# Four conditioned transformer layers in one recorded schedule: values by twos, layer 3 rebuilt, minima, tables on GpSimd, and products of the identity in TensorE's waits

## The chip, the cores and the metric

The kernel runs on one core of one Trainium2 chip, in one launch. The metric is device time in microseconds (us), the median of the runs shown. The engines are TensorE (PE; its weight loads, PEld, are listed apart), VectorE (DVE), ScalarE (ACT), GpSimd (POOL), and SyncE (SP), whose queue issues most DMAs.

## The reference, cut to what matters

Four layers follow each other on x of shape (4, 512, 512), all in float32; a conditioning vector of 512 numbers per batch element scales and shifts inside them.

```
# layer 0: attention, 16 query heads of 32, 4 key heads; keys and values through a latent of 128
h = layernorm(x) * (1 + scale) + shift           # scale, shift from the conditioning
q, k = rope(h @ Wq.T), rope((h @ Wkd.T) @ Wku.T); v = (h @ Wkd.T) @ Wvu.T
x = x + softmax(masked(q k^T / sqrt(32))) v @ Wo.T      # a window of +-64 and every 64th key
# layer 1: attention, 8 query heads of 64, one key head; then a gated MLP of 2048
h = rms(x) * w * (1 + scale);   x = x + softmax(rope(q) rope(k)^T / 8) v @ Wo.T
h = rms(x) * w2 * (1 + scale2); x = x + (silu(h @ Wg.T) * (h @ Wu.T)) @ Wd.T
# layer 2: attention with normalized q and k, 16 heads of 32, an additive bias; then an MLP of 2048
q, k = q / |q| * sm, k / |k|;   x = x + (softmax(q k^T + bias) v @ Wproj.T + bproj) * gamma1
x = x + (gelu_tanh(h @ Wfc1.T + bfc1) @ Wfc2.T + bfc2) * gamma2
# layer 3: 8 experts on slices of 64 features, then a projection
y = gelu(x_e @ W1[e] + b1[e]) @ W2[e] + b2[e]            # e = 0..7, hidden 256
hn = (layernorm(y) * g + b) * (1 + scale) + shift
x = x + silu(hn) @ out_W + out_b
```

## The kernel before, in words

**Two streams, one recorded order.** Each of the four batch elements passes the stages `a01` (attention of layers 0 and 1), `m1` (MLP of layer 1), `a2` (attention of layer 2) and `m2` (MLP of layer 2 and the experts of layer 3). Two streams run side by side: `STREAM_A` holds mostly attentions, `STREAM_M` mostly MLPs. At the start both are in `a01`, of elements 1 and 0; at the end element 3's experts are done in two halves, one per stream. The stages are Python generators. They yield a cost, or an `Until`, which says when a buffer is written or free. `interleave` picks the next step of a stream, and the class `Clocks` keeps a plan: it knows about when each engine will be done with each tile. Every instruction is recorded with its planned start and emitted sorted by it, so that the order on each engine is written out before the kernel runs and nothing reorders it on the chip. Where no step is ready, `interleave` moves the planned time of TensorE (`clocks.now`) forward to the earliest `Until`.

**Lines of the profile.** All work goes through four helpers, so line numbers tell the helper and the tile names tell the step: L301 is every operation of VectorE, ScalarE and GpSimd, L354 every matrix product (`mm`), L360 every transpose by TensorE (`tr`, a product with the identity `ident`), L367 the loads on SP's queue (`load`).

**Tiles.** 512 tokens are 4 tiles of 128 rows. Stream A's names are `nq` (normalized input, then transposed queries), `h`, `probs`, `pT`, `kT`, `v`, `wa_*` (weights); stream M uses `mn`, `mT`, `wm`, `hid`, `x` and `wm_*` for the same things. A side has two PSUM banks of its own, `bank`; scores go to `two`, two pairs of banks that both sides share. `late` is a scratch of VectorE, then a ring of conditioning weights, then the additive bias of layer 2.

**Attention.** A unit is one block of heads (`c`) and one tile of queries (`qt`). `attention` goes through the units: it issues the scores of the next unit, then `back` transposes the probabilities of this one (TensorE into a bank, copied to `pT` by `evict`, which takes ScalarE or VectorE, whichever the plan has free first), and `values` multiplies `pT` by `v` into a bank, evicted to `ctxT`. The list `late` holds units whose values are outstanding; with two in it the older is done:

```
            if len(late) == 2:
                yield Until(*when, side.at, of=late[0][1])
                values(*late.pop(0))
```

Scores use a quarter (32 rows) or a half (64) of the array, four or two at a time; values a quarter or half of the columns.

**Softmax.** `maxima` adds the bias and takes the row maximum on VectorE, negates it in a second operation, and `soften` lets ScalarE exponentiate with it and sum, VectorE invert the sums and GpSimd multiply.

**Tables.** `tables` and `trig` make sines and cosines for rope with some 20 operations; table "0" (128x64) and table "1" (128x512) both on VectorE, at the start. The conditioning weights are loaded into `late` after table "1".

**Layer 2's q, k, v** are made in that order, four token tiles each; q and k are squared on ScalarE, summed on VectorE, and scaled on GpSimd. **Layer 3** (`experts`) adds the first bias in `first` on VectorE and ScalarE, applies Gelu in place over all of `hid`, transposes back in `third`, normalizes, turns with `turned`, applies Silu in place, and projects.

Of the kernel before, what the change touches and what calls it, by code (L numbers as in the profile page):

```python
# [12 lines left out]
F32 = mybir.dt.float32  # L13
# [11 lines left out]
LOWEST = -3.0e38  # L25
# [283 lines left out]
def cond_seq_kernel(ctx: ExitStack, tc: tile.TileContext, a: dict, out: bass.AP):  # L309
# [89 lines left out]

    class Side:  # L400
# [8 lines left out]
        def bank(self):  # L409
            return clocks.tile(self.row_tag + "bank", 2, self.pools[0], (P, 512), "bank", name("bank"))  # L410

        def at(self, k=1):

            return clocks.free(self.row_tag + "bank", 2, k)
# [12 lines left out]
    class AttentionSide(Side):  # L427
# [28 lines left out]
        def pair(self):  # L456
            t = two_banks()
            return [t[:, 0, :], t[:, 1, :]]

        def pair_at(self):  # L460
            return clocks.free("two", 2)

    class OtherSide(Side):
# [25 lines left out]

        def pair(self):  # L490
            return [self.bank(), self.bank()]

        def pair_at(self):
            return self.at(2)
# [72 lines left out]
    def trig(ang, k, e, sin, nsin, cos):  # L567


        r = ang  # L570

        def nearest(period):
            vector.tensor_scalar(k, r, 1.0 / period, MAGIC, ALU.mult, ALU.add)
            vector.tensor_scalar(k, k, -MAGIC, None, ALU.add)

        def less(part):
            vector.scalar_tensor_tensor(r, k, -part, r, ALU.mult, ALU.add)

        far = TWO_PI * 2.0**17
        big = split(far, 2.0**8, 12, 2)  # L580
        nearest(far)
        less(big[0])
        less(big[1])
        vector.tensor_scalar(e, k, big[2], None, ALU.mult)
        nearest(TWO_PI)
        for part in split(TWO_PI, 2.0**-4, 7, 4):
            less(part)
        vector.tensor_tensor(r, r, e, ALU.subtract)
        nearest(TWO_PI)
        for part in split(TWO_PI, 2.0**-9, 12, 2):  # L590
            less(part)
        vector.tensor_scalar(r, r, PI_F32, -PI_F32, ALU.min, ALU.max)
        scalar.activation(e, r, AF.Abs)
        scalar.activation(sin, r, AF.Sin)
        scalar.activation(cos, e, AF.Sin, bias=half_pi, scale=-1.0)
        vector.tensor_scalar(nsin, sin, -1.0, None, ALU.mult)

    def tables(label, n, half, tokens, freqs):
# [3 lines left out]
        vector.tensor_tensor(  # L602
# [5 lines left out]
        parts = [const.tile([P, n * half], F32, name=f"{label}_{i}") for i in range(3)]  # L608
        trig(ang, k, e, *parts)
        return [t.rearrange("p (t i) -> p t i", i=half) for t in parts]  # L610
# [31 lines left out]
    def norm_steps(n, src, eps, rms=False, tiles=range(NT)):  # L642

        mv, own = tiny([P, NT, 2], "mv"), slice(tiles[0], tiles[-1] + 1)
        for t in tiles:
            st = tiny([P, 6], "st")
            vector.bn_stats(st, src[:, t, :])
# [83 lines left out]
    def maxima(p, s, bias, width, scale):  # L731

        mx = tiny([P, 2], "mx")
        for j in range(2):
            vector.tensor_tensor_reduce(
                out=p[:, j, 0:width], in0=s[:, j, 0:width], in1=bias, scale=scale, scalar=LOWEST,
                op0=ALU.add, op1=ALU.max, accum_out=mx[:, j : j + 1],
            )
        neg = tiny([P, 2], "neg")
        vector.tensor_scalar(neg, mx, -1.0, None, ALU.mult)  # L740
# [4 lines left out]
    def attention(side, units, scores, back, values, work, first, final=True):  # L745
# [15 lines left out]

        yield Until(scorable, of=first)
# [3 lines left out]
        for i, u in enumerate(units):  # L766
            cost, more = 0.0, i + 1 < len(units)
            when = [scorable] if more else []
            if len(late) == 2:
                yield Until(*when, side.at, of=late[0][1])  # L770
                values(*late.pop(0))
                cost += work[1]
            else:
                yield Until(*when)
# [9 lines left out]
        for u, pT in late:  # L784
            yield Until(side.at, of=pT)
            values(u, pT)
            yield work[1]
# [81 lines left out]
    coefs, tabs, ended = {}, {}, set()  # L869
# [16 lines left out]
    def attention0(b, side):  # L886
# [4 lines left out]
        if "0" not in tabs:  # L891
            tabs["0"] = tables("tab0", NT, 16, tok, freq[:, 32:48])
# [61 lines left out]
        def scores(u):  # L954
# [11 lines left out]
            for q, sc in zip(p, s):  # L966
                neg = maxima(q, sc, bias, n, 1.0 / math.sqrt(32.0))
                soften(q, q, neg, n, 1.0)
# [19 lines left out]
        def values(u, pT):  # L988
            c, qt = u
            (pT,), o, bl = pT, side.bank(), blocks(qt)  # L990
            for i, (at, n) in enumerate(bl):
                for g in range(4):
                    mm(
                        o[quarter(g), 0:P], lhsT=v[0:n, qt, i, quarter(g)],
                        rhs=pT[0:n, i, g * P : (g + 1) * P], start=i == 0, stop=i == len(bl) - 1,
                    )
            evict(ctxT[:, c, qt * P : (qt + 1) * P], o[:, 0:P])

        if "1" not in tabs:

            posf = const.tile([P, B * NT], F32, name="posf")
            vector.tensor_copy(posf, pos_i)
            tabs["1"] = tables("tab1", B * NT, 32, posf, freq[:, 0:32])
            ringC.load(1)
# [6 lines left out]
    def attention1(b, side):  # L1011
        n, wkv1 = side.n(), (yield from unit_for(b, "wkv1"))
        norm(n, xs[b], 1e-6, rms=True)
        yield from known("n1")
        hT = side.h()
# [66 lines left out]
        def values(u, pT):  # L1082
            c2, qt = u
            o = side.bank().rearrange("p (i q) -> p i q", q=P)
            for i in range(2):
                for at in range(NT):
                    for j in range(2):
                        mm(
                            o[half(j), i, :], lhsT=v[:, at, :], rhs=pT[i][:, j, at, :],
# [599 lines left out]
```

## Time and profile before

| | |
|---|---|
| median of 3 runs | 2498.31 us (2492.44 to 2498.45) |
| the profiled execution | 2497.25 us |
| its span, first to last instruction | 2495.5 us |
| TensorE | 2432.5 us busy (97%), 12564 instructions |
| VectorE, ScalarE, GpSimd | 1190.5, 877.6, 733.5 us busy |
| mean granted clock of TensorE | 0.992 |
| moved by DMA | 154.18 MB, 62 GB/s on average |

A product in float32 is two records in the profile, a transpose is one. Busy times count a record from its start to its modelled end, so two records that overlap count once. An idle time is put down to the instruction whose semaphore ended it. A time before or after the span (1.75 us here) belongs to the execution as well.

### The profile page before, as it was taken

The page shows a single profiled execution, that of the slowest core. Times are in us where ns is not written, and L with a number is a line of the kernel's source. Part 1 is how long each engine was busy: PE and PEld are TensorE (multiplying, and loading weights), DVE is VectorE, ACT ScalarE, POOL GpSimd, SP SyncE. Part 2 cuts the span into 40 slices and gives each one's busy share as a digit, 9 for nine tenths or more (in the row PEclk, how much of TensorE's full clock was granted, in tenths as well). Part 3 has the DMA queues.
Part 4 walks back from the last instruction along what each step waited for, and adds up shares of the span by engine and source line. Part 5 has one row for each costly group of instructions (what it writes and reads, how often), then busy time and mean ns, then how long its engine had stood idle before and what let it go on. Part 6 is the DMA issues. An engine that isn't in the chain of part 4 may idle for free.

```text
span 2495.5 us, 33420 instructions
## 1 busy us (share of the span) xinstructions
PE 2432.5 (97%) x12564; PEld 1242.0 (50%) x12564; DVE 1190.5 (48%) x3180; ACT 877.6 (35%) x2071; POOL 733.5 (29%) x921
## 2 busy tenths in 40 slices
PE   7989999999999999999999999999999999999997
PEld 4555655444554555554455455554455444554443
DVE  6766552133654454625554455443465333763233
ACT  2645441002551351414353043333255202651233
POOL 2433320005332223324222232424332205533221
PEclk9999999999999999999999999999999999999998
DMA  3220122220113111111211111112111221102210
GB/s 112 100 74 18 52 68 68 86 87 34 35 52 106 51 52 55 39 68 55 89 48 61 63 69 65 42 56 72 68 35 52 83 89 53 44 32 95 72 55 21
DMA packets 83312, 154.18 MB, mean 62 GB/s; under 512 B 3584, under 2 KB 10784, under 8 KB 83152
## 3 DMA queue, kind: packets, MB, share of 16 engines
q1 hardware_dynamic: 82544, 151.83, 17.9%
q8 instruction: 100, 1.64, 0.3%
q14 instruction: 60, 0.49, 0.1%
q0 software_dynamic: 176, 0.15, 0.1%
q10 hardware_dynamic: 432, 0.07, 0.0%
HBM read 147.83 MB, written 4.21 MB: 61 GB/s over the span
## 4 chain that ended last, share of the span: by engine, by line
PE 88%; DVE 3%; issue 3%; ACT 2%; POOL 2%; DMA 1%; ACTq 0%; POOLq 0%; DVEq 0%
PE bank L354 71%; PE bank L360 11%; PE two L354 6%; POOL inv L301 1%; ACT probs L301 1%; DVE probs L301 1%; ACT wm L301 0%; DVE neg L301 0%; POOL t L301 0%; DVE pT L301 0%; DMA late_ada_g<-in_units 0%; DMA wm<-in_units 0%; DVE t L301 0%; DMA late_ada_t<-in_units 0%; POOL probs L301 0%
## 5 line engine op out<-in xcount | busy, mean ns | idle before, releaser
L301 POOL TENSOR_SCALAR probs<-probs,inv 128x512 f32<-128x512 f32 (+4 forms) x544 | 316.4, 596 | 688.4 <-DVE inv L301 579.4
L301 ACT ACTIVATE probs<-probs,neg 128x512 f32<-128x512 f32 (+2 forms) x448 | 265.4, 594 | 254.8 <-DVE neg L301 254.3
L360 PEld LDWEIGHTS bank<-ident,probs 128*128 128x128 f32 (+2 forms) x1744 | 201.9, 141 | 161.9 <-issue 128.6
L360 PE MATMUL bank<-ident,probs 128*128 128x128 f32 (+2 forms) x1744 | 245.4, 276 | 4.1 <-ACT arow L301 1.2
L354 PE MATMUL bank<-mT,wm_gate 128*128 128x512 f32 x512 | 248.9, 597 | 0.0
L354 PE MATMUL bank<-mT,wm_up 128*128 128x512 f32 x512 | 245.7, 597 | 0.0
L354 PE MATMUL bank<-wm_down,hid 128*128 128x512 f32 x512 | 239.6, 596 | 0.7 <-DVE hid L301 0.7
L301 DVE CUSTOM_DVE_ANT_0 probs<-two,late 128x512 f32<-128x512 f32 x256 | 166.2, 686 | 74.3 <-PE two L354 56.4
L354 PE MATMUL bank<-wm_fc,hid 128*128 128x512 f32 x384 | 187.6, 594 | 0.0
L354 PE MATMUL bank<-mT,wm_fc 128*128 128x512 f32 x384 | 182.6, 597 | 0.0
L301 ACT COPY pT<-bank 128x512 f32<-128x512 f32 (+2 forms) x240 | 133.8, 580 | 83.8 <-PE bank L360 75.8
L354 PEld LDWEIGHTS bank<-pT,v 128*32 128x32 f32 (+2 forms) x3488 | 110.7, 116 | 95.9 <-issue 33.3
L354 PE MATMUL bank<-pT,v 128*32 128x128 f32 (+2 forms) x3488 | 146.0, 278 | 8.3 <-DVE pT L301 5.8
L301 ACT ACTIVATE mt<-bank 128x512 f32<-128x512 f32 x64 | 37.8, 591 | 327.6 <-PE bank L354 327.6
L354 PE MATMUL bank<-wa_q,h 128*128 128x512 f32 x320 | 152.4, 599 | 0.2 <-DVE t L301 0.2
L301 DVE TENSOR_TENSOR x<-x,bank 128x512 f32<-128x512 f32 x100 | 68.4, 684 | 176.1 <-PE bank L354 176.0
L354 PE MATMUL two<-kT,nq 32*128 32x512 f32 (+5 forms) x1088 | 150.0, 539 | 1.1 <-DVE mx L301 1.1
L354 PEld LDWEIGHTS bank<-wm_down,hid 128*128 128x128 f32 x512 | 91.7, 190 | 98.1 <-issue 96.2
L354 PEld LDWEIGHTS bank<-mT,wm_up 128*128 128x128 f32 x512 | 91.0, 190 | 98.2 <-issue 97.7
L301 DVE RECIPROCAL inv<-total 128x2 f32<-128x2 f32 x320 | 53.0, 166 | 172.9 <-ACT probs L301 155.7
L354 PEld LDWEIGHTS bank<-mT,wm_gate 128*128 128x128 f32 x512 | 90.0, 190 | 90.8 <-issue 90.3
L301 DVE COPY pT<-bank 128x512 f32<-128x512 f32 (+2 forms) x199 | 131.1, 680 | 5.9 <-PE bank L360 5.0
(221 smaller groups left out, 3396.3 us busy)
## 6 DMA issues: line engine op xcount, KB each, us to landing
wm_fc<-in_units SPq DMA_DIRECT2D x24, 1024.0 KB, 5.6
wm_gate<-in_units SPq DMA_DIRECT2D x16, 1024.0 KB, 5.7
wm_up<-in_units SPq DMA_DIRECT2D x16, 1024.0 KB, 5.7
wm_down<-in_units SPq DMA_DIRECT2D x16, 1024.0 KB, 5.4
wa_q<-in_units SPq DMA_DIRECT2D x10, 1024.0 KB, 5.5
wa_fc<-in_units SPq DMA_DIRECT2D x8, 1024.0 KB, 5.5
wa_o<-in_units SPq DMA_DIRECT2D x6, 1024.0 KB, 5.7
wa_k<-in_units SPq DMA_DIRECT2D x4, 1024.0 KB, 5.6
```

What stands on the lines that cost most here:

```text
L301: return call(*map(real, args), **{k: real(x) for k, x in kw.items()})
L354: latest[0] = nc.tensor.matmul(real(out), lhsT=real(lhsT), rhs=real(rhs), **kw)
L360: latest[0] = nc.tensor.transpose(real(out), real(src), unit)
```

## The change

The new parts, each with what it does:

- `attention` does the values of two units together, when both have their `pT`; each `values` writes both into one bank (256 columns) and evicts once.
- `maxima` becomes `lowest`: scores times minus the scale, the row minimum; it goes to the exponential as it is (`scale=-1.0`), and the negation is gone.
- `trig` and `tables` take an engine and yield between operations. Table "0" stays on VectorE; table "1" goes to GpSimd as a list of `chores`, one operation at a time, whenever its input is ready in the plan. [...] Layer 1 of element 0 and the loads of the conditioning weights wait for that table.
- Layer 2's products come as q0 to q3, k0, k1, v0, k2, v1, k3, v2, v3; k is evicted by the freer engine, and VectorE does the scaling.
- Layer 3: `first` takes pairs of `two` on both sides and lets Gelu read PSUM with its bias; statistics are taken per block of 128 columns as they come; Silu becomes z(1 + tanh z) with z half of the input (the coefficients are halved once), per block.
- A side may take a bank of `two` for its own work when no attention is in its scores and its own banks are free later.
- `keep_up`: before `interleave` moves the planned time forward by a wait, it issues products of the identity with itself into a free bank, as many as fit the wait less 0.4 us at 0.215 us each, when that is at least two. Nothing reads them. The changed program has 117, in 21 places.

```diff
 class Side:
         def bank(self):
+            if not scoring and clocks.now < self.own() > clocks.free("two", 2):
+                return two_banks()[:, 0, :]
+            return self.own_bank()
...
+    def trig(ang, k, e, sin, nsin, cos, engine):
...
         def less(part):
-            vector.scalar_tensor_tensor(r, k, -part, r, ALU.mult, ALU.add)
+            if engine is vector:
+                vector.scalar_tensor_tensor(r, k, -part, r, ALU.mult, ALU.add)
+            else:
+                engine.tensor_scalar(sin, k, -part, 1.0, ALU.mult, ALU.mult)
+                yield Until(of=[sin])
+                engine.tensor_tensor(r, r, sin, ALU.add)
+            yield Until(of=[r])
...
-    def maxima(p, s, bias, width, scale):
-        mx = tiny([P, 2], "mx")
+    def lowest(p, s, bias, width, scale):
+        neg = tiny([P, 2], "neg")
         for j in range(2):
             vector.tensor_tensor_reduce(
-                out=p[:, j, 0:width], in0=s[:, j, 0:width], in1=bias, scale=scale, scalar=LOWEST,
-                op0=ALU.add, op1=ALU.max, accum_out=mx[:, j : j + 1],
+                out=p[:, j, 0:width], in0=s[:, j, 0:width], in1=bias, scale=-scale, scalar=HIGHEST,
+                op0=ALU.add, op1=ALU.min, accum_out=neg[:, j : j + 1],
             )
-        neg = tiny([P, 2], "neg")
-        vector.tensor_scalar(neg, mx, -1.0, None, ALU.mult)
         return neg
...
     def attention(side, units, scores, back, values, work, first, final=True):
...
             if len(late) == 2:
-                yield Until(*when, side.at, of=late[0][1])
-                values(*late.pop(0))
-                cost += work[1]
+                yield Until(*when, side.at, of=late[0][1] + late[1][1])
+                values(late)
+                late = []
+                cost += 2 * work[1]
...
     def attention0(b, side):
         if "0" not in tabs:
-            tabs["0"] = tables("tab0", NT, 16, tok, freq[:, 32:48])
+            for _ in tables("0", NT, 16, tok, freq[:, 32:48], vector):
+                pass
+            posf = const.tile([P, B * NT], F32, name="posf")
+            vector.tensor_copy(posf, pos_i)
+            chores.append(tables("1", B * NT, 32, posf, freq[:, 0:32], gpsimd))
...
     def attention2(b, side):
-        for which, dst in (("q2", qT), ("k2", kT)):
+        for which, t in [("q2", 0), ("q2", 1), ("q2", 2), ("q2", 3), ("k2", 0), ("k2", 1)] + [
+            x for i in range(2) for x in (("v2", i), ("k2", i + 2))
+        ] + [("v2", 2), ("v2", 3)]:
...
-                gpsimd.tensor_tensor(qv, qv, inv.unsqueeze(2).to_broadcast([P, 16, 32]), ALU.mult)
+                vector.tensor_tensor(qv, qv, inv.unsqueeze(2).to_broadcast([P, 16, 32]), ALU.mult)
...
-        def values(u, pT):
-            c, qt = u
-            o = side.bank()
-            for at in range(NT):
-                for g in range(4):
-                    mm(
-                        o[quarter(g), 0:P], lhsT=v[:, at, c * P + 32 * g : c * P + 32 * g + 32],
-                        rhs=pT[g // 2][:, g % 2, at, :], start=at == 0, stop=at == NT - 1,
-                    )
+        def values(two):
+            o, (c, first) = side.bank(), two[0][0]
+            for k, (_, pT) in enumerate(two):
+                for at in range(NT):
+                    for g in range(4):
+                        mm(
+                            o[quarter(g), k * P : (k + 1) * P],
+                            lhsT=v[:, at, c * P + 32 * g : c * P + 32 * g + 32],
+                            rhs=pT[g // 2][:, g % 2, at, :], start=at == 0, stop=at == NT - 1,
+                        )
...
     def experts(b, side, tiles=range(NT)):
-                for j in range(2):
-                    bias = V_B1 + 4 * p + 2 * j + f
-                    if j == 0:
-                        vector.tensor_scalar(at(j, f), s[j][:, 0:n], vec[:, bias : bias + 1], None, ALU.add)
-                    else:
-                        scalar.activation(at(j, f), s[j][:, 0:n], AF.Identity, bias=vec[:, bias : bias + 1])
-            for h in hid:
-                scalar.activation(h[:, :, 0:n], h[:, :, 0:n], AF.Gelu)
+            for f in range(2):
+                for j in range(2):
+                    bias = V_B1 + 4 * p + 2 * j + f
+                    scalar.activation(at(j, f), bank(j, f), AF.Gelu, bias=vec[:, bias : bias + 1])
...
+            for t in tiles:
+                vector.bn_stats(stats[:, t, p, :], y[:, t, p * P : (p + 1) * P])
...
-        yield from turned(side, y, hT, b, coefs["gain"], coefs["lift"], tiles)
-        scalar.activation(hT[:, :, lo : lo + n], hT[:, :, lo : lo + n], AF.Silu)
+        for c in range(NC):
...
+            scalar.activation(h, ps, AF.Tanh, bias=lift, scale=gain)
+            vector.tensor_scalar(z, ps, gain, lift, ALU.mult, ALU.add)
+            vector.scalar_tensor_tensor(h, h, 1.0, z, ALU.add, ALU.mult)
...
+    def keep_up(until):
+        start = max(clocks.now, clocks.written(ident))
+        count = int((until - start - 0.4) / 0.215)
+        if count > 1:
+            rings = [] if scoring else [("two", two_banks)]
+            rings += [(side.row_tag + "bank", side.own_bank) for side in (sideA, sideM)]
+            for ring, make in rings:
+                if clocks.free(ring, 2) <= start:
+                    p = make()
+                    p = p[:, 0, 0:P] if ring == "two" else p[:, 0:P]
+                    for _ in range(count):
+                        mm(p, lhsT=ident, rhs=ident, start=True, stop=True)
+                    break
...
             elif cond and cond_until.time < min(s.until for s in live):
+                keep_up(cond_until.time)
                 clocks.now = cond_until.time
             else:
                 s = min(live, key=lambda s: s.until)
+                keep_up(s.until)
                 clocks.now = max(clocks.now, s.until)
                 s.step()
```

## The prediction

> **What bounds the kernel now.** I read the page first, then busy time by stretches, then TensorE's timeline in the middle, then the clock around the slow stretches, then the tail. The page gives the bound:
>
> ```profile
> PE 2432.5 (97%) x12564; PEld 1242.0 (50%) x12564; DVE 1190.5 (48%) x3180; ACT 877.6 (35%) x2071; POOL 733.5 (29%) x921
> PEclk9999999999999999999999999999999999999998
> ```
>
> TensorE (PE) is busy 97% of 2495.5 us, no other engine half of it: PE is idle for 63.0 us. The stretches tell where (columns: stretch and its length, then busy us and count of PE, weight loads, VectorE, ScalarE, GpSimd; the granted clock; DMA share; GB/s):
>
> ```profile
> 0.00:100.00 100.00, 83.06 (x518) 48.19 (x522) 69.61 (x237) 41.53 (x125) 34.84 (x68) 0.98 0.33 100
> 100.00:200.00 100.00, 89.94 (x825) 54.11 (x816) 66.25 (x321) 55.80 (x208) 38.48 (x87) 0.97 0.23 78
> 200.00:300.00 100.00, 94.59 (x679) 58.35 (x679) 57.92 (x136) 47.52 (x128) 35.54 (x52) 0.98 0.13 43
> 300.00:400.00 100.00, 94.35 (x628) 57.00 (x625) 48.75 (x92) 39.07 (x97) 22.68 (x33) 0.98 0.13 43
> 400.00:1100.00 700.00, 698.21 (x3254) 349.92 (x3253) 304.50 (x797) 198.59 (x492) 171.82 (x217) 1.00 0.19 64
> ...
> 2400.00:2496.00 96.00, 81.50 (x289) 36.01 (x287) 31.60 (x61) 29.16 (x47) 21.56 (x18) 0.90 0.08 28
> ```
>
> Idle are 38.1 us in the first 400 (two attentions side by side, VectorE 49 to 70% busy), 14.0 in the tail, and only 10.9 in the 2000 us between. There the end moves by what PE's own work costs. The timeline shows that this is more than products (start, length, group; the next start matters, since lengths hold a tail of 0.17):
>
> ```profile
> 611.02 10.47 PE L354 MATMUL bank<-wa_v,h 128*128 128x512 f32 x24
> 621.33 0.60 PE L360 MATMUL bank<-ident,t 128*128 128x128 f32 x4
> ...
> 640.28 2.74 PE L354 MATMUL bank<-mT,wm_up 128*128 128x512 f32 x6
> 642.95 1.08 PE L354 MATMUL bank<-pT,v 128*32 128x128 f32 x32
> 643.96 1.14 PE L354 MATMUL two<-kT,nq 32*128 32x512 f32 x8
> 645.03 1.09 PE L360 MATMUL bank<-ident,probs 128*128 128x128 f32 x8
> ```
>
> 24 records from 611.02 to 621.33 are 0.429 us each, two to a product of 512 columns: 0.86. Values (pT,v) and scores (kT,nq) fill the array four at a time, so each of these two groups is worth 0.86 too; but from start to next start they take 1.01 and 1.07. The excess, 0.15 and 0.21, is paid where products of one tile size (128*128, 128*32, 128*64, 32*128, 64*128) follow another. I call it a switch. By kind its median in the trace is 0.15 to 0.22; before has 663, worth 127 us. Products at steady rates are 2260 us; the rest of the busy time is slow clock and tails.
>
> **Switches: the main term.** Values by twos halve the groups of values: 160 before, 80 after, each with the same products. A scores-then-values round had three switches; every other round now has two. In the order of the changed program PE has the same 7674 products and transposes plus 117 fillers, and 522 switches. Each kind's count times its median gives 127.2 before, 101.8 after: **-25.4**. Nearly all of it lies where PE does not wait, so it is on the path. Ends: 141 fewer at 0.15 or at 0.21, -21 to -30.
>
> What it adds is a wait: both units' pT, the second transposed just before. The copy to pT takes 0.59 on ScalarE or 0.68 on VectorE, with 0.17 of PE's tail and hops about 0.95. Queued behind on PE is everything, as its order is fixed. But in that order at least 1.05 us of PE's work stands between the pair's last transposes and its first value product for 79 of the 80 pairs, mostly two products of the other stream (1.72); the 80th has 0.46. I take 0; without that cover it costs 80 x 0.95 = 76. Halved copies of values leave VectorE and ScalarE, beside PE.
>
> **Fillers and the clock.** 117 products of the identity, in 21 places: 23 before the first product, 3 before the first product of q0, 37 in 8 places of the two-attention phase, 18 in 4 places of the middle, 36 in 4 places at the end. Each is two records of 128 columns, so 0.215 at full clock, 0.43 at half. The clock in stretches of one window, same columns, each pair before and in a slow one:
>
> ```profile
> 60.60:64.00 3.40, 1.92 (x10) 0.63 (x8) 3.33 (x14) 2.19 (x6) 1.26 (x1) 1.00 0.66 216
> ...
> 347.30:350.70 3.40, 0.77 (x8) 0.53 (x5) 3.09 (x8) 2.90 (x9) 1.08 (x2) 1.00 0.00 0
> ```
>
> ```profile
> 64.00:67.40 3.40, 3.15 (x9) 1.73 (x8) 3.05 (x17) 2.31 (x11) 2.38 (x5) 0.50 0.27 98
> ...
> 350.70:354.10 3.40, 3.35 (x32) 3.28 (x32) 0.68 (x2) 0.47 (x1) 1.61 (x3) 0.50 0.02 5
> ...
> 2473.80:2487.50 13.70, 8.37 (x15) 3.80 (x16) 2.55 (x7) 3.47 (x4) 0.71 (x1) 0.50 0.00 0
> ```
>
> A stretch with PE 0.77 to 1.92 of 3.4 us busy is followed by 3.4 us at 0.50. There are six such stretches before the tail (23.9 us, PE busy 23.6 of it) and 13.7 in the tail (busy 8.4). Half of the busy time is lost: 11.8 + 4.2. The first weight products, 16 records in 8.70 us at 22.76, lose 8.70 - 6.87 = 1.8. In all 17.8. The fillers stand in just such waits, but shorter waits have none: I take **-12**, ends 0 and -18.
>
> [...] The trace shows 0.50 after single waits of at most 2.7 us. [...]
>
> A filler that starts while the next operand is already there delays everything by itself. The identity is ready at 1.4 us and the first product starts at 9.27; 23 fillers between them take 4.9 at full clock, 9.9 at half, so at half they end 2.0 late: I take 1. The 91 after these 26 cost 19.6 at full clock; their cover is the waits of PE, and I take a tenth, 2. Together **+3**, ends 0 and +22.
>
> **Tables on GpSimd.** For layer 1 VectorE drops 10 operations at 0.69, 8 at 0.42, 2 at 0.69 and one at 0.43: 12.1 us between 24 and 60. GpSimd gains 10 at 1.27 and 17 at 0.60: 22.9 in the same phase, where it is busy 35 to 38%; its rope sums (1.27) and softmax products queue behind one such step at a time, up to 1.3 each. Conditioning's loads now wait for the tables, and SP's queue has them later; what needs all coefficients, layer 2, comes after 600 us.
>
> **Minima, and the start's waits.** The minimum in place of the maximum drops 256 negations at 0.17 and puts the result straight before ScalarE's exponential. No row shows the min form; its nearest, the max form, is 0.69 at 512 columns, and I take the same. In the middle it is beside PE. In the first 400 us, 64 of them (11 us) and the tables' 12 leave VectorE, 23 of its 242 busy us, a tenth. Waits there, 38.1 idle less 9.3 before the first product, are 28.8; a tenth of these is 3, and free "two" banks that a side may now use when nobody scores remove some more: **-8**, ends +10 (GpSimd's queue) and -20.
>
> **Layer 2's order, layer 3.** PE waits 2.0 us near 1165 and 1763 for GpSimd's scaling of k (1.05 on GpSimd, 0.69 on VectorE after). Values products between the k tiles cover a part, but fillers still stand there: 0. Layer 3 drops VectorE's additions and ScalarE's in-place pass; Gelu reads PSUM, four at about 0.59 (nearest row, Tanh from PSUM), 2.4, in place of an addition of 0.6 and one Gelu of 1.91: the consumer gets it as late as now, and PE has the other stream. Its "two" pairs are shared with scores; ends -3 and +8, taken 0. Only the tail is bare:
>
> ```profile
> 2471.53 0.44 PE L360 MATMUL bank<-ident,t 128*128 128x128 f32 x2 [0.22 <-DVE t L301]
> ...
> 2472.41 0.69 DVE L301 BATCH_NORM_STATS2 st<-nq 128x6 f32<-128x512 f32 x1 [0.94 <-ACT nq L301]
> ...
> 2479.11 1.28 ACT L301 ACT_TABLE_LOAD   x1 [0.49 <-DVE h L301]
> 2480.40 1.06 ACT L301 ACTIVATE h<-h 128x1024 f32<-128x1024 f32 x1
> 2481.51 10.07 PE L354 MATMUL bank<-wm_out,h 128*128 128x512 f32 x16 [3.06 <-ACT h L301]
> ```
>
> Two statistics of 0.69 shrink to two of 128 columns (between 0.17 and 0.69). From the first transposes to the last products 4.8 pass now; after: load 1.28, four Tanh at 0.56, one step of 0.5, 4.0. Together **-1**, ends -2 and +1.
>
> **Sum.** -25.4 - 12 + 3 - 8 - 1 = -43.4 against the profiled execution of 2497.25 (span 2495.5): 2453.9. It is 1.1 under the median of 2498.31, so about **2455**.
>
> **Rivals.**
> 1. *Values wait for the newest pT* (slower). At 0.95 for a bare pair, 80 bare cost 76: 2455 + 76 = 2531. It decides from 43.4 / 0.95 = 46 bare pairs of 80. For it: the wait is real. Against: 1.05 or more at 79 pairs. 0.06.
> 2. *Fillers are bare.* 91 x 0.215 = 20 instead of 3, and the clock gains little: -25 - 6 + 20 - 1 = -12, with the start unchanged: 2486. For it: nothing on PE can pass them. Against: in before, waits of 1 to 4 us stand at the same steps. 0.12.
> 3. *The clock is not theirs to raise*: the stretches at 0.50 follow waits too short for a filler, and 0 to 4 of the 12 come: 2463 to 2467. For it: a wait under about 0.8 gets none. Against: most slow stretches follow a longer one. 0.15.
> 4. *The start opens up*: waits there fall by 20 rather than 8, all slow stretches go: 2455 - 12 - 6 = 2437. For it: VectorE is busiest there. 0.17.
> 5. The change not doing what it says is left out by the order: 80 groups, 522 switches, 117 fillers are in it.
>
> **Numbers.** My case, 2446 to 2463, has 0.50. A range from 2434 to 2481 leaves out the slower rival, half of rival 2 and the far end of 4, under 0.2. The measurement of this kernel tells about 0.3%, 7.5 us, from no change. Faster by more: 0.50 + 0.17 + 0.15 + 0.09 = 0.91; within: 0.04 (rivals 1 and 2 in part); slower: 0.05.
>
> **What would show it.** Right: a pT,v group of 64 records taking about 1.87 to the next start, idle PE unchanged in the middle, the clock at 1.00 through 64, 350 and 1767 and in the tail, PE's busy sum lower by some 20 although 25 of fillers are in it. Wrong: waits of bank<-pT,v for ScalarE or VectorE copies above 10 us in all; fillers directly followed by products that waited for nothing; slow stretches that remain; GpSimd's queue ending waits of the softmax in the first 100 us.

## The result, and the profile after

| | before | after |
|---|---|---|
| median of 6 runs (lowest to highest) | 2494.90 us (2491.28 to 2498.45) | 2477.23 us (2475.66 to 2481.23) |
| ratio, 95% interval | | 0.9932 (0.9917 to 0.9946) |
| profiled execution, its span | 2497.25, 2495.5 | 2475.82, 2474.0 |

The change gains 17.7 us where 43 were forecast: right in its sign, 22 us from the number, and outside 2446 to 2463, which had half the chance. The first section of the page gives busy time and instructions by engine, the line below it the granted clock in 40 slices:

```profile
PE 2427.1 (98%) x12798; PEld 1278.0 (52%) x12798; DVE 1124.0 (45%) x2903; ACT 864.5 (35%) x2075; POOL 726.6 (29%) x920
PEclk9999999999999999999899999999999999999999
```

TensorE's sum fell by 5.4, not by some 20, and there is a new slow slice, the twentieth. The stretches (length, then busy us and count of PE, weight loads, VectorE, ScalarE, GpSimd; granted clock; DMA share; GB/s) show where:

```profile
0.00:100.00 100.00, 91.23 (x664) 56.88 (x664) 62.08 (x238) 48.55 (x151) 65.34 (x109) 0.97 0.30 90
...
400.00:1100.00 700.00, 696.99 (x3271) 352.77 (x3270) 297.11 (x733) 200.36 (x490) 169.54 (x214) 1.00 0.18 62
1100.00:1200.00 100.00, 87.95 (x312) 42.80 (x311) 40.48 (x85) 30.73 (x50) 29.10 (x14) 0.93 0.23 77
1200.00:2400.00 1200.00, 1194.55 (x6108) 606.10 (x6107) 542.07 (x1326) 424.16 (x937) 356.58 (x412) 1.00 0.18 61
2400.00:2474.00 74.00, 64.30 (x316) 36.58 (x314) 24.19 (x59) 23.64 (x53) 13.04 (x12) 1.00 0.06 22
```

Between 1100 and 1200 TensorE is idle for 12 us at a mean clock of 0.93. The same stretch of before:

```profile
1100.00:1200.00 100.00, 96.87 (x330) 43.95 (x329) 44.80 (x85) 35.12 (x45) 43.70 (x26) 1.00 0.15 53
```

TensorE's waits of after (tile, releaser: us in total, times, longest) say that it is one wait:

```profile
PE bank L360 <- DVE t L301: 12.7, 4, 11.6
PE bank L360 <- DVE pT L301: 6.0, 20, 0.3
PE two L354 <- ACT hid L301: 3.1, 3, 1.9
```

Its cause is three queues away. TensorE's timeline of after has the last products of the keys (`wa_k`), ended at about 1171.6, and the wait for `t`, the scaled keys:

```profile
1168.01 3.60 PE L354 MATMUL bank<-wa_k,h 128*128 128x512 f32 x8
1178.75 1.88 PE L354 MATMUL bank<-mT,wm_up 128*128 128x512 f32 x4
1192.26 1.09 PE L360 MATMUL bank<-ident,t 128*128 128x128 f32 x4 [11.63 <-DVE t L301]
```

VectorE, which makes `t`, stood for 15.89 at the statistics of `x`, the next element's input, which are ahead of it in VectorE's order:

```profile
1169.54 0.69 DVE L301 TENSOR_TENSOR t<-t,inv 128x512 f32<-128x512 f32 x1 [3.02 <-POOL inv L301]
1186.12 0.69 DVE L301 BATCH_NORM_STATS2 st<-x 128x6 f32<-128x512 f32 x1 [15.89 <-DMA x<-in_x]
```

And `x` was late because of SP's queue, where it stood behind a load that waited:

```profile
1129.94 0.37 SPq L367 DMA_DIRECT2D wa_v<-in_units  x1
1171.64 0.37 SPq L367 DMA_DIRECT2D wa_proj<-in_units  x1
1172.10 2.73 SPq L301 DMA_DIRECT2D out<-x  x4
1180.68 0.39 SPq L367 DMA_DIRECT2D x<-in_x  x1
```

Nothing was issued between 1130 and 1171: `wa_proj` overwrites the keys' weights, and with keys and values interleaved the last key product ends only then (1168.01 and 3.60 above). Behind it stood the four stores of element 0, and behind these the load of element 3's `x`, which takes element 0's place and so waits until the stores have landed. The load had been recorded when the values' weights are taken, before the last two key products were planned, so the plan held the buffer for free and put the load ahead of the stores.

### The profile page after: what moved, and what is told of

The parts are those of the page before. It is cut to its first block, busy times and chain, and to the rows that moved or that the text cites. A ratio compares the mean times of both kernels' runs of the same rounds, so it can differ in the third digit from the quotient of the medians.

```text
span 2474.0 us, 33722 instructions
## 1 busy us (share of the span) xinstructions
PE 2427.1 (98%) x12798; PEld 1278.0 (52%) x12798; DVE 1124.0 (45%) x2903; ACT 864.5 (35%) x2075; POOL 726.6 (29%) x920
## 4 chain that ended last, share of the span: by engine, by line
PE 93%; DVE 3%; ACT 2%; issue 1%; DMA 1%; POOL 0%; SPq 0%; DVEq 0%; ACTq 0%; POOLq 0%
PE bank L354 70%; PE two L354 11%; PE bank L360 11%; DVE probs L301 1%; DVE pT L301 1%; PE two L360 0%; ACT probs L301 0%; ACT wm L301 0%; DVE nq L301 0%; DMA out<-x 0%; DMA x<-in_x 0%; DMA wm<-in_units 0%; DVE mt L301 0%; ACT pT L301 0%; ACT L301 0%
## 5 line engine op out<-in xcount | busy, mean ns | idle before, releaser
L354 PE MATMUL bank<-mT,wm_gate 128*128 128x512 f32 x512 | 247.8, 595 | 0.0
L354 PE MATMUL bank<-mT,wm_up 128*128 128x512 f32 x512 | 246.9, 599 | 0.0
L354 PE MATMUL bank<-wm_down,hid 128*128 128x512 f32 x496 | 232.5, 597 | 0.0
L354 PE MATMUL bank<-wm_fc,hid 128*128 128x512 f32 x384 | 189.5, 593 | 0.0
L354 PE MATMUL bank<-mT,wm_fc 128*128 128x512 f32 x384 | 183.0, 595 | 0.0
L301 ACT COPY pT<-bank 128x512 f32<-128x512 f32 (+3 forms) x258 | 145.2, 577 | 81.1 <-PE bank L360 72.3
L354 PE MATMUL two<-kT,nq 32*128 32x512 f32 (+5 forms) x1088 | 149.7, 537 | 0.4 <-DVE neg L301 0.4
L354 PEld LDWEIGHTS bank<-mT,wm_up 128*128 128x128 f32 x512 | 91.3, 191 | 100.1 <-issue 99.6
L354 PEld LDWEIGHTS bank<-pT,v 128*32 128x32 f32 (+2 forms) x3488 | 113.0, 116 | 49.0 <-issue 20.9
L354 PEld LDWEIGHTS bank<-mT,wm_gate 128*128 128x128 f32 x512 | 90.5, 190 | 91.3 <-issue 91.3
L354 PEld LDWEIGHTS bank<-wm_down,hid 128*128 128x128 f32 x496 | 89.0, 190 | 94.2 <-issue 92.9
L301 POOL TENSOR_TENSOR inv<-ss,neg_half 128x16 f32<-128x16 f32 x32 | 92.8, 2901 | 131.1 <-DVE ss L301 131.1
L354 PE MATMUL bank<-pT,v 128*32 128x128 f32 (+2 forms) x3488 | 130.4, 274 | 0.0
L301 POOL TENSOR_TENSOR rstd<-var,neg_half 128x4 f32<-128x4 f32 (+1 forms) x25 | 24.7, 992 | 359.3 <-DVE var L301 359.1
L354 PE MATMUL bank<-wa_q,h 128*128 128x512 f32 x272 | 129.9, 596 | 0.0
```

Of the source, the lines that this page charges most:

```text
L301: return call(*map(real, args), **{k: real(x) for k, x in kw.items()})
L354: latest[0] = nc.tensor.matmul(real(out), lhsT=real(lhsT), rhs=real(rhs), **kw)
```

## Experiments

In the tables a difference is between two medians, each of 4 to 11 runs whose spread is 2 to 8 us; below 2 us it tells nothing. The runs were made in several rounds, in which before itself had medians of 2493.4 to 2495.8; differences of the ratios to before are within 1.4 us of those in the tables. "Useful work" is the sum of TensorE's steady durations without fillers (0.429 us per record of 512 columns, times the share of the array that its tile fills), 2256 us in every version. Compared at equal useful work, a profile tells in which stage a difference arose.

**First four: the wait, and two parts alone.**

`a_hold_k`, in the ring's bookkeeping:

```diff
 weights[which] = side.ring.take(which)
+if which == "k2":
+    side.ring.held[side.ring.taken - 1] = which
...
+if which == "k2" and t == NT - 1:      # after the last key product
+    side.ring.held = {at: x for at, x in side.ring.held.items() if x != "k2"}
+    side.ring.load(side.ring.taken + 1)
```

> The changed kernel, where the buffer of the key weights of layer 2 counts as held until the last key product is recorded; so the load of the projection weights (wa_proj) into it stands behind the four stores of element 0 and the load of x for element 3 in SP's queue, not ahead of them. Theory A (SP's queue: a load that waits 41 us for TensorE stood at its head, x of element 3 came late and VectorE's statistics with it): the wait of 11.6 us of bank<-ident,t at 1180 goes, with it the slow clock of 1183 to 1197 (about 2): about 2463 us, 12 to 14 below the changed kernel; the load of x lands before 1170. Rival B (VectorE's order itself, the statistics standing ahead of layer 2's keys, is what costs): x lands earlier, yet the wait stays above 8 us and the time within 4 of the changed kernel, 2474 or more.

`a_qkv_order`:

```diff
-for which, t in [("q2", 0), ... ("k2", 1)] + [x for i in range(2) for x in (("v2", i), ("k2", i + 2))] + ...
+for which, t in [(w, i) for w in ("q2", "k2", "v2") for i in range(NT)]:
```

> The changed kernel, where layer 2's products come in the old order again (q0 to q3, k0 to k3, v0 to v3); scaling on VectorE and all else stay. Theory A (the new order of q, k, v is what put the load of the projection weights in front of SP's queue): the wait of 11.6 us near 1180 goes, but the waits of TensorE for the scaled k (about 2 us in each of three middle elements, partly taken by fillers) come back: 2466 to 2470. Rival B (the order is not the cause): the long wait stays, 2477 or more.

`b_twos`: the kernel before with the new `values` and `yield Until(..., of=late[0][1] + late[1][1])`.

> The kernel before, with values by twos alone; 568 switches of tile size instead of 663 by its order. Theory A (a switch costs TensorE 0.15 to 0.21 us wherever TensorE does not wait): 95 x 0.17 = 16 less, about 2479. Rival B (the pairs wait for the newer pT and give it back): 2486 to 2495, with waits of bank<-pT,v for ScalarE or VectorE of 8 us or more in all. Rival C (a switch costs nothing of its own, the longer group is only a tail in the records): 2492 to 2495, with no such waits.

`b_fill`: the kernel before with `keep_up` and its two calls.

> The kernel before, with the products of the identity alone (150 in 29 places, into a side's own banks only). Theory A (they keep the granted clock up in the middle and in the tail, and some delay the next product): stretches at 0.50 near 350, 1767 and 2453 to 2487 gone, about 9 us, less 2 to 4 where they are bare: 2486 to 2489. Rival B (bare): no gain or slower, 2494 to 2505, with fillers followed at once by products that waited for nothing. Rival C (the clock follows something else): the stretches at 0.50 stay, 2492 to 2500.

| | median | ratio to before |
|---|---|---|
| after | 2477.23 | 0.9932 (0.9917 to 0.9946) |
| a_hold_k | 2464.92 | 0.9877 (0.9863 to 0.9891) |
| a_qkv_order | 2464.22 | 0.9881 (0.9865 to 0.9897) |
| b_twos | 2487.46 | 0.9972 (0.9961 to 0.9983) |
| b_fill | 2490.02 | 0.9982 (0.9974 to 0.9991) |

SP's queue of a_hold_k issues the stores 15 us and `x` 11 us sooner, `wa_proj` 3 later:

```profile
1133.34 0.37 SPq L367 DMA_DIRECT2D wa_v<-in_units  x1
1156.99 10.64 SPq L301 DMA_DIRECT2D out<-x  x4
1169.43 0.39 SPq L367 DMA_DIRECT2D x<-in_x  x1
1175.04 0.39 SPq L367 DMA_DIRECT2D wa_proj<-in_units  x1
```

The long wait is gone, as TensorE's waits of a_hold_k show,

```profile
PE bank L360 <- DVE t L301: 1.1, 3, 0.4
```

and 12.3 us with it: theory A, although `x` landed only at about 1174.6 and not before 1170. TensorE has the same records in the same order in both kernels, so its own work is not what differs. Undoing the order of q, k, v gives the same 13.0; the waits for scaled keys that I expected back did not come.

Values by twos alone gave 6 of 16: the number is rival B's, but not the waits of 8 us that belong to it. At equal useful work the middle (400 to 2200 us of it) gained 6.9 where its fewer switches are worth 11.6. Of the 4.7 that are missing, 0.9 are idle time of TensorE (11.9 there, 11.0 in before), 0.3 of it before products of values; where the rest went is open. The start gained 1.5 where its switches are worth 4.5; the mean granted clock of the whole profile is 0.991, of before's 0.992.

Fillers alone gave 3.4. The time at half clock fell from 55 to 23 us (this counts the start as well, where no granted clock is on record yet but records of 512 columns take 0.85 us, twice the later 0.43), but fillers of 32 us took the place of waits.

**Next four, each an edit of a_hold_k.**

`h_tail_rev`, in `first` of layer 3, for the halves:

```diff
-for f in range(2):
-    for j in range(2):
+for f in range(2) if n == S else (1, 0):
+    for j in range(2) if n == S else (1, 0):
         scalar.activation(at(j, f), bank(j, f), AF.Gelu, ...)
```

> a_hold_k, where the four Gelus of a half of layer 3 (two tiles, one pair of two for all four blocks) are recorded last block first, so that by the order of the kernel the fourth product no longer waits for the first Gelu, which reads another part of the same pair. Theory A (these waits of two<-h,wm_exp and two<-mT,wm_exp, about 7.5 us in the last 70, are what took the gain of the tail): 2457 to 2460 against 2464.9 of a_hold_k. Rival B (ScalarE's chain of Gelus sets the tail, and the same time comes back where the second product waits for them): 2463 to 2466.

`h_no_fill`, in `keep_up`: `if count > 1` becomes `if False`.

> a_hold_k without the products of the identity. Theory A (the forecast: the clock they keep up is worth 12 and they cost 3): 2472 to 2476. Rival B (they pay with their own length for what the clock wins, as 3.4 us gained by 150 of them in the kernel before suggest): 2462 to 2469. Stretches at 0.50 should be back near 350, 1767 and in the tail in either case.

`h_singles`: `values([late.pop(0)])` in place of `values(late)`.

> a_hold_k with the values one unit at a time again (99 switches more by its order). Theory A (all of a switch's 0.17 lies on the path): 2480 to 2484. Rival B (half of it is given back as waits, as in the kernel before with values by twos alone, which gained 6 of 16): 2470 to 2475.

`h_tab_vec`: `tables("1", ..., gpsimd)` becomes `tables("1", ..., vector)`.

> a_hold_k with table 1 on VectorE again, as chores between its other work. Theory A (VectorE holds the start back, and 12 us less on it are worth a tenth to a third): 2466 to 2470, the difference made in the first 400 us. Rival B (the start is set by other waits): 2462 to 2466. Rival C (GpSimd's queue delays the softmax there more than VectorE is relieved): below 2462.

| | median | against a_hold_k |
|---|---|---|
| h_tail_rev | 2456.96 | -8.0 |
| h_no_fill | 2462.99 | -1.9 |
| h_singles | 2475.17 | +10.2 |
| h_tab_vec | 2467.69 | +2.8 |

The tail is theory A. TensorE's timeline of after in it (6 records of 256 columns go, 2 wait for the first Gelu):

```profile
2445.44 1.13 PE L354 MATMUL two<-h,wm_exp 64*128 64x256 f32 x6
2447.19 0.70 PE L354 MATMUL two<-h,wm_exp 64*128 64x256 f32 x2 [0.62 <-ACT pT L301]
2447.82 1.08 PE L354 MATMUL bank<-pT,wm_exp 128*64 128x256 f32 x8
```

and of h_tail_rev, where the eight go together:

```profile
2423.61 1.13 PE L354 MATMUL two<-h,wm_exp 64*128 64x256 f32 x8
2424.68 1.08 PE L354 MATMUL bank<-pT,wm_exp 128*64 128x256 f32 x8
```

Six such waits were 0.56 to 1.90 each. The Gelu reads another part of the same pair, but the order is kept for the whole pair: in the written order the first Gelu stands between the third product and the fourth, so the fourth waits for it.

The fillers are worth nothing (rival B): without them the slow clock is back in the tail (0.90 from 2390 to 2465, 0.98 in a_hold_k), but the time is not. Near 350 (1.00 from 300 to 400) and 1767 it is not back, against what I expected in either case, so there the fillers are not what removed it.

h_singles lies just above the range of its rival B: 10.2 of 17. At equal useful work its middle is 12.5 slower for 11.9 of switches, all of it, and its start 3 faster.

Tables on GpSimd are worth 2.8 by the medians, but the intervals of the two ratios overlap (0.9874 to 0.9899, and 0.9863 to 0.9891), and the profiles do not put a gain in the first 400 us (there they differ by some 2 the other way; the mean granted clocks of the profiles are 0.996 and 0.995).

**Third four, each an edit of h_tail_rev.**

`t_latest`:

```diff
-latest[0] = nc.tensor.matmul(...)
+made = nc.tensor.matmul(...)
+if lhsT is not ident:
+    latest[0] = made          # what the next load waits for
```

> h_tail_rev, where a load no longer waits for products of the identity. (Each load waits for the TensorE product emitted last before it; with 23 products of the identity in front, the first loads of x and of the conditioning weights left SP's queue at 2.23 and 7.2 to 8.4 us instead of 0.73 and 2.58, in all seven kernels that have them and in none of the three that don't.) Theory A (this is what delays the start): the loads leave at 0.73 and 2.58 again, the first product of wm,cT starts at 9.3 instead of 10.8 to 12.1, and the time is 2453 to 2455.5 against 2457.0 of h_tail_rev. Rival B (the start is set by VectorE and the coefficients behind it, not by its loads): 2456 to 2458.

`t_tail_fill`: `if count > 1 and clocks.now > 2300.0` in `keep_up`.

> h_tail_rev with the products of the identity in the last 4 of their 21 places only. Theory A (before the tail they pay with their own length and the late loads for what the clock wins): 2452 to 2456, below 2457.0. Rival B (the clock they keep up in the start and the middle is worth more): 2459 to 2463.

`t_no_fill`: `if False` there.

> h_tail_rev without any product of the identity. Theory A (in the tail the 36 there are worth about 2.5: the clock at 0.50 over 13.7 us costs more than their length): 2455 to 2459, 2 to 4 above the kernel with those of the tail alone. Rival B (worth nothing in the tail either): within 1 of the kernel with those of the tail alone.

`t_negs`:

```diff
+vector.tensor_scalar(neg, low, 1.0, None, ALU.mult)     # low: the row minimum
```

> h_tail_rev with a small operation of VectorE (128 rows by 2, 0.17 us) put back between the row minimum and the exponential, 256 times, where the kernel before has its negation. Theory A (the minima relieve VectorE and shorten the chain in the start, where scores wait for it, a part of the forecast's 8): 2459 to 2462, made in the first 400 us. Rival B (beside TensorE everywhere): 2456 to 2458. Rival C (it also gives back waits in the middle, as values by twos alone did): above 2462, made between 400 and 2300.

| | median | against h_tail_rev |
|---|---|---|
| t_latest | 2455.52 | -1.4 |
| t_tail_fill | 2454.94 | -2.0 |
| t_no_fill | 2454.34 | -2.6 |
| t_negs | 2462.74 | +5.8 |

The start of after, first SP's queue, then TensorE:

```profile
2.23 4.66 SPq L367 DMA_DIRECT2D x<-in_x  x4
7.46 5.96 SPq L367 DMA_DIRECT2D wm<-in_units  x7
```

```profile
1.41 7.36 PE L354 MATMUL two<-ident 128*128 128x128 f32 x46 [1.41 <-POOL ident masks.py:199]
10.80 0.43 PE L354 MATMUL bank<-wm,cT 128*32 128x128 f32 x8 [2.04 <-DVE late L301]
```

and of t_latest:

```profile
1.41 7.99 PE L354 MATMUL two<-ident 128*128 128x128 f32 x46 [1.41 <-POOL ident masks.py:199]
9.33 0.43 PE L354 MATMUL bank<-wm,cT 128*32 128x128 f32 x8
```

With the first fillers the first product came 1.5 later than in before, though they had ended 2 us ahead of it: the loads had waited for them (`load` makes a DMA wait for the last TensorE product written before it). In t_latest the loads leave at 0.73 and 2.59 and the product at 9.33. So the mechanism is shown; that it is worth time is not, since the median moved by 1.4 and this profile had the clock at 0.50 for twice as long in the start (its mean granted clock is 0.996, that of h_tail_rev 0.999). Fewer fillers are no worse: with those of the tail alone 2.0 less, without any 2.6 less, neither much beyond the spread, so those of the tail bring nothing either (rival B of t_no_fill). The dummy operation of t_negs cost 5.8, 0.7 more than theory A has, and made in the first 300 us of useful work as that theory says (12 in the two profiles). The fillers grew to 26 places and 32 us with it, 6.6 of these in that stretch, so what the operation costs without fillers is open.

**Last three, each an edit of t_no_fill.**

`u_qkv`: the edit of a_qkv_order in place of the held buffer. `u_singles`: that of h_singles. `u_pool_scale`:

```diff
-vector.tensor_tensor(qv, qv, inv..., ALU.mult)
+gpsimd.tensor_tensor(qv, qv, inv..., ALU.mult)
```

> t_no_fill with layer 2's products in the old order q, k, v in place of the held buffer: a version that leaves out the products of the identity and the new order, and has the last block's Gelu first. Theory A (the new order of layer 2 brings nothing once its load is in place): 2453 to 2456, as t_no_fill (2454.3). Rival B (values between the keys cover waits for their scaling): 2457 to 2460.

> t_no_fill with the values one unit at a time again, about 100 switches more, and no products of the identity that change their number with it. Theory A (all of a switch's 0.17 is on the path): 2470 to 2474 against 2454.3. Rival B (a third to a half comes back: without pairs TensorE waits less for copies of pT): 2463 to 2468.

> t_no_fill with layer 2's scaling of q and k on GpSimd again (32 operations of 1.05 there, 0.69 on VectorE). Theory A (the forecast: the waits for it near 1165 and 1763 are as long as before, 0): 2453.5 to 2455.5 against 2454.3. Rival B (moving it took waits of TensorE away, 2 us in each of three middle elements): 2457 to 2461.

| | median (lowest to highest) | ratio to before | against t_no_fill |
|---|---|---|---|
| u_qkv | 2453.21 (2448.87 to 2457.17) | 0.9830 (0.9809 to 0.9851) | -1.1 |
| u_singles | 2467.12 (2461.93 to 2469.33) | 0.9883 (0.9862 to 0.9903) | +12.8 |
| u_pool_scale | 2465.35 (2462.63 to 2467.48) | 0.9879 (0.9857 to 0.9900) | +11.0 |

The surprise is the last. TensorE's waits of u_pool_scale have

```profile
PE bank L360 <- POOL t L301: 6.4, 3, 3.0
```

and behind two of the three the clock is at 0.50 for 3.4 us, near 1140 and 1734. At equal useful work it falls 3.0, 3.3 and 1.3 us back in the three places and hardly elsewhere; 8 of the 11 are in the profile, some 3 of them as waits and 3.4 as work at half clock. t_no_fill waits 4.0 there for VectorE, but keeps its clock; before had 6.0 there for GpSimd. So the scaling on VectorE is what shortened the waits of before near 1165 and 1763; the new order beside it brought nothing (u_qkv). All this is without fillers; no run has them and the scaling on GpSimd. u_singles is slower by 12.8 with 93 switches more, 0.14 for each, within its rival B's range; its middle pays in full here too (12.8 at equal useful work).

The best versions, t_no_fill and u_qkv, are 40 us faster than before and 23 faster than after. They leave out the fillers, have layer 2's load behind the stores or the old order, and the last block's Gelu first.

## Why the prediction was wrong, step by step

- **Layer 2's order, taken 0: the step that failed most.** "Its load" was never walked past SP's queue. Interleaving k and v moved the last use of the keys' weights behind the place of a load that waits for it, and the load held the stores, the next `x`, VectorE's statistics and TensorE: +12.3. In the same step the scaling on VectorE was put at nothing and is worth -11.0 in the kernel without fillers (u_pool_scale). In the changed kernel, where fillers stand in those waits, its worth was not measured; a part of the 11 is the clock, which fillers could have kept up. So two errors of opposite sign, and how nearly they cancel is not shown.
- **The clock, -12, and fillers, +3: together 9 forecast, nothing came** (+1.9 with them in a_hold_k against h_no_fill, +2.6 in h_tail_rev against t_no_fill). The stretches at 0.50 near 350, 1767 and in the tail did go (1.00 in after from 300 to 400 and from 1200 on), but the first two are gone without fillers too. The fillers paid with their own length, which I put at a tenth, they held the first loads, and in the start slow stretches remained (0.50 behind 12.4, 104.5, 125.0 and 241.1). I had also read the stretches ahead of a slow one as 0.77 to 1.92 of 3.4 us busy; the one at 104.9 in before was busy for 2.42, with no wait above 1.12, so a long wait was not what they had in common; and the slow clock of the tail came behind a single wait of 3.87. Rival 2 had this mechanism (bare fillers, 0.12); its 2486 missed the rest, and no run shows the 6 that it has for the clock: in the versions tried with and without fillers, those with them were 1.9 and 2.6 longer.
- **Layer 3, taken 0 within -3 to +8, the tail -1.** "PE has the other stream" failed: the fourth product's wait for the first Gelu stands inside a group, where TensorE's order has no product of the other stream; with the Gelus turned, 8.0 us go (h_tail_rev). That is a price within the new version. Against before, from 2200 us of useful work on, the profile of after is 2.3 shorter with the clock up, and that of h_no_fill, about as long at half clock as before, 0.2 longer, though fewer switches should save it 3.4 there. So in the tail layer 3 as a whole cost some 3 by this estimate, within -3 to +8: what it dropped paid for most of that wait.
- **Switches, -25.4.** The mechanism was right: a group of 64 records of values now takes 1.88 to the next start, where two groups took 2 x 1.01, and with the twos undone the middle gave back all that its switches are worth (12.5 for 11.9 in h_singles). a_hold_k, without the long wait, gained 17.7 in the middle at equal useful work, where its switches are worth 18.5; but the scaling and the clock changed there too. TensorE's timeline of after:

```profile
641.80 1.95 PE L354 MATMUL bank<-pT,v 128*32 128x128 f32 x64
643.68 1.14 PE L354 MATMUL two<-kT,nq 32*128 32x512 f32 x8
```

  Undone, the twos cost 10.2 and 12.8 where the medians gave 17 and 16: what is missing is missing in the start, where the profiles without them are 3 and 1.5 faster; whether waits or the clock there made that is not shown. The other 42 switches were not tried alone. Alone in the kernel before the twos gave only 6; why 4.7 are missing in its middle is open.
- **The start, -8.** The medians have it in sum: minima 5.8, tables 2.8. But the second is not seen in the start of its profile and the first was taken with more fillers, so that the sum fits is in part luck.
- **Values wait for the newest pT (rival 1): no.** In after all waits of L354's `bank` for a copy of pT are 1.8 us together.

The gain fell short by some 25 us. Two steps, each measured next to the changed kernel, make up 21 to 23 of it: 12.3 for the load in layer 2, and 9 to 11 for the clock and the fillers, where 9 were forecast and nothing, or a loss of 2, came. What is left over holds terms of opposite sign (the switches, the scaling, layer 3, the start) that were measured in different versions, so they are not added up.

## What to carry to other kernels

Where an edit moves the last use of a buffer, walk every load that overwrites it through its queue, and everything behind it: here SP's queue, in its order, turned one wait on a weight that nobody needed yet (from 1130 to 1171.64) into a wait for data that somebody did (15.89 us of VectorE, 11.63 of TensorE). A product that nothing reads was not free even in a wait: it takes its own length when the plan's wait is longer than the real one (in b_fill 32 us of them, with 32 us less at half clock, gained 3.4), and what counts "the last product" counts it too (here the loads, the first of which left at 2.23 and not at 0.73). Before you sum forecasts, look for steps put at nothing because two effects in them seem to cancel: price each by itself.

## What the runs showed of the hardware

**The slow stretches lie on a grid of 3.41 us.** In the profiles of before and of after, all edges of the slow stretches within them lie on one grid of 3.413 us, within 0.02. Its place against the first instruction differs between executions: the first such edge stands 2.55 us past a multiple of 3.413 in before (63.99) and 2.13 in after (12.37), and about 1.6 and 0.1 in the two that follow. a_hold_k and h_tail_rev have the same TensorE order in the start; their stretches (columns as above) are

```profile
8.40:11.80 3.40, 0.58 (x14) 0.23 (x14) 2.85 (x12) 0.00 (x0) 1.39 (x2) 1.00 1.00 294
11.80:28.90 17.10, 15.54 (x98) 11.14 (x99) 5.86 (x26) 5.08 (x11) 5.81 (x9) 0.50 0.74 202
```

and

```profile
10.40:13.80 3.40, 0.85 (x16) 0.34 (x16) 2.52 (x11) 0.37 (x1) 2.66 (x4) 1.00 1.07 298
13.80:20.60 6.80, 6.25 (x51) 5.00 (x51) 2.85 (x14) 1.52 (x3) 1.89 (x3) 0.50 0.86 222
```

One has 17 us at half clock there, the other 7, and at 400 us of useful work the second is 5.9 ahead. So a few us between two profiles in the start need not be the edit.

**TensorE's first records took twice their time.** In before, products of 512 columns at 23.6 us still take 0.85 us a record, and 0.43 from about 26.4, where the granted clock goes on record. In after, whose fillers begin at 1.41, that is at 5.5: a record of 128 columns takes 0.21 up to there and 0.11 behind it. The views count the time ahead of it as full clock (1.00 from 0 to 26.40 in before).

**In before and after, the work in a step of that grid went with the clock better than busy time did.** In after, TensorE was 2.78 of 3.40 us busy from 121.6 and still got 0.50 from 125.0:

```profile
121.60:125.00 3.40, 2.78 (x37) 2.15 (x30) 2.78 (x14) 2.89 (x12) 1.72 (x5) 1.00 0.82 278
125.00:128.40 3.40, 3.40 (x17) 3.40 (x18) 1.98 (x12) 1.93 (x9) 2.30 (x6) 0.50 0.08 31
```

I took each record's columns at 0.429 us per 512, times the share of the array that its tile fills, over the windows (steps of the grid) on record at full clock in before and after. The 12 followed by 0.50 held 0.13 to 0.36 of a window's work; of the 1411 followed by full clock, 3 held 0.37 or less. A limit on busy time that takes in all 12 (0.83 of a window) takes in 31 of the others. That window of after held 0.36: among its records are eight of 4 columns (0.95 us busy) and eights of 32 rows (0.61), which keep TensorE busy and count for little in this sum. Weighted by the tile's rows alone, a limit of 0.51 takes in the 12 and some 7 others; unweighted, the 12 reach up to 0.95. So this is a measure that fits these two profiles, not a rule. The window from 121.6 had no long idle time either: 0.62 us of 3.40. From these counts I estimate that a filler raises the clock where it lifts its own window over about 0.37; as the grid's place differs between executions, which window that is differs too. No run was made to test this alone.
